# LSTM over 512 steps with a residual: opening matmuls, head sums on GpSimd, and the order of loads at the end

## The chip, the cores and the metric

The kernel runs on one core of a Trainium2 chip. The core has five engines that work at the same time, each with its own stream of instructions: PE (TensorE, matmuls), DVE (VectorE), ACT (ScalarE), POOL (GpSimd) and SP (SyncE, which here only issues DMAs). They wait for each other by semaphores. All arithmetic is in float32. The metric is the device time of one execution in microseconds.

## The reference

```python
xW = jnp.einsum('ntd,dg->ntg', x, Wx) + b       # x: (32, 512, 512), Wx: (512, 2048)
def step(carry, xw_t):
    prev_h, prev_c = carry
    a = xw_t + prev_h @ Wh                       # Wh: (512, 2048)
    i = sigmoid(a[:, :Hd]);  f = sigmoid(a[:, Hd:2 * Hd])
    o = sigmoid(a[:, 2 * Hd:3 * Hd]);  g = tanh(a[:, 3 * Hd:])
    next_c = f * prev_c + i * g
    next_h = o * tanh(next_c)
    return ((next_h, next_c), next_h)
_, hs = jax.lax.scan(step, (h0, zeros), swapaxes(xW, 0, 1))
out = x + swapaxes(hs, 0, 1)                     # batch 32, 512 steps, width 512
```

Two matrix products carry the arithmetic: x by Wx, which does not depend on the recurrence, and h by Wh, which must be done step after step.

## The kernel before

**Two kinds of PE work.** In every step t, `h_part(t)` (L245) adds h by Wh into the step's PSUM bank `gbank`; the profile shows it as 32 records of 128x512 elements. The product x by Wx is made ahead of the recurrence and put between the h_parts, so that PE has work while ACT and DVE run the step's `cell` (L260 to L271: sigmoids, tanh, products, and a transpose that gives the new h, `ht`). GpSimd adds x to h for the output (`oc`, L279).

**The stream.** For steps 20 to 499, x by Wx is computed with a fast bilinear algorithm that needs fewer products. The steps come in 20 groups of 24; a group has 20 slots, a slot seven products (L516). Each product has

- a left operand, a sum of rows of x: rows are loaded into `xs` (L475, alternately in `xs0` and a part of `r1`), four "pair sums" per group (`pair_sum`, L480 to 486, 128x768) follow, then "U sums" (`u_op`, L424, 128x896, into the six buffers of `ubuf`, made by `u_ahead` as far as the next matmuls need them);
- a right operand, a sum of blocks of Wx ("V rows"), made once in the first 90 us, stored to `vdram` and read back row by row into the three places of `vring` (L595, `load_v_ahead`), always three rows at most.

The products gather in five PSUM banks `xbank` and in `bbank`. `evacuate` (L562 to 578) copies and adds them into `cbuf`; `needs` says which evacuation must have been issued before a bank is used again. "W sums" (`w_op`, L389, 128x1024 in `cbuf`) then form the blocks of x by Wx, which are stored to `xwd` (L405) and come back per step into `xw` (L613, four loads, three steps ahead); ACT copies `xw` into the bank of the next step (`seed_step`, L624). Some banks start from a bias row rather than from zero: `seed_banks` (L546) copies one of six "seeds". The six are differences of the four bias rows in two halves; two are made early (`early_seeds`), four late (`late_seeds`: three 256 KB loads by POOL at L729, three splits L733, three sums L741 to 743 on DVE).

**The head.** Steps 0 to 19 use plain products (`plain_block`, L178): those of five steps stand ahead of the loop, the rest in the loop's steps 0 to 7. Before those, a loop of three rounds with four matmuls each (L795) multiplies a zeroed tile into banks that are not in use yet. From step 7 on the head's steps run the stream, in chunks of up to 24 quarter products; each chunk loads V rows, makes U sums, evacuates, makes W sums as long as the budget `room["dve"]` lasts, and issues the matmuls; after the first chunk of a step comes its `cell`.

**The main loop and the end.** From step 16 on each step has one run of stream matmuls, and the same calls in a fixed order: evacuate, seeds, V loads, U sums, pair sums, W sums, matmuls, cell. The stream ends at step 472 (`END`) and 473; steps 500 to 511 use plain products again (`plain_part`, L187), which are put into steps from 472 on, 10 per step until `SPLIT` (474) and 5 after. From 474 on a step's gates are worked on in two halves. The x rows for the output come in chunks of eight steps (`load_x`, L151); the last chunk is loaded into a place that served as a spare `cbuf` buffer.

**The order** of each engine's instructions is the order of these calls: nothing reorders them. SP issues all DMAs but three, in one queue; an issue whose data or place is not ready holds up every issue behind it. At the end of a step's `h_part`, SP gets the stores of the step before, then the x chunk if one is due, the `xw` loads, and later the V loads.

Of the kernel before, what the change touches and what calls it, by code (L numbers as in the profile page):

```python
# [12 lines left out]
P = 128  # L13
# [7 lines left out]
W = G * P  # L21
HW = G * H
# [56 lines left out]
def cost_dve(cols):  # L79
    return 150 + 1.05 * cols  # L80
# [17 lines left out]
def kernel(  # L98
# [193 lines left out]

    free_c = list(range(NC))
    last_x = []
    free_u = list(range(6))
    room = {"dve": 0.0}
# [5 lines left out]
    def flat(a):  # L304
        return a.rearrange("p a b -> p (a b)")
# [110 lines left out]
    def u_block(gr, i):  # L416
        if i < 6:
            return flat(xs[gr.g % 2][:, i, 1:8])
        return flat(ubuf[:, gr.u[i]])

    def u_op(gr, terms):
        (a, sa), (b, sb) = sorted(terms.items(), key=lambda v: -v[1])
        dst = take(free_u)
        (add if sb > 0 else sub)(flat(ubuf[:, dst]), u_block(gr, a), u_block(gr, b))  # L424
        room["dve"] -= cost_dve(896)
        for i in (a, b):
            if i > 5:
                gr.u_uses[i] -= 1
                if gr.u_uses[i] == 0:
                    free_u.append(gr.u[i])  # L430
        return dst

    u_made = [0]

    def make_sum(gr, i):
        if i > 5 and i not in gr.u:
# [36 lines left out]
            in_=xg[g].rearrange("p (k s m) -> p k s m", k=6, s=4),  # L473
        )

    def pair_sum(g, i):
        z = xs[g % 2]
        a21, a11, a12, a22, s1, s2, s3, s4 = (z[:, :, n] for n in range(8))
        if i == 0:
            add(s1, a21, a22)  # L480
        elif i == 1:
            sub(s2, s1, a11)
        elif i == 2:
            sub(s3, a11, a21)
        else:
            sub(s4, a12, s2)
        room["dve"] -= cost_dve(768)
# [5 lines left out]
                items.append((row, row - back, r))  # L493
    pos = [0]
    finished = []

    def emit_matmuls(n):

        while n > 0 and pos[0] < 4 * len(items):
            i, q = divmod(pos[0], 4)  # L500
            row, slot, r = items[i]
            gr, s = group(slot // R), slot % R
            xb = xbank[slot % 5]
            if q == 0 and any(f in finished for f in needs(slot, r)):
                evacuate()
            if r == 2:
                dst = bbank[:, slot % 2 * HW : (slot % 2 + 1) * HW]
            elif r in (5, 3):
                dst = xb[:, HW:W]
            else:  # L510
                dst = xb[:, 0:HW]
            start = q == 0 and (r == 2 or (r == 1 and s not in BIAS_OF))
            size = 4 if q == 0 and n >= 4 else 2
            cols = slice(q * HW // 4, (q + size) * HW // 4)
            for j in range(4):
                nc.tensor.matmul(  # L516
                    dst[j * B : (j + 1) * B, cols],
                    left_of(gr, s, r)[:, j * B : (j + 1) * B],
                    vring[:, row % 3, RIGHT[r], cols],
                    start=start,  # L520
                    stop=True,
                    skip_group_check=True,
                )
            pos[0] += size
            n -= size
            if pos[0] % 4 == 0:
                finished.append((slot, r))
                if r == 4:
                    left_done(gr, s)
# [205 lines left out]
    def early_seeds():  # L735
        split_seeds((4, 5))
        sub(seeds[5], seeds[5], seeds[4])

    def late_seeds():
        split_seeds((0, 1, 2))  # L740
        add(seeds[3], seeds[2], seeds[4])  # L741
        sub(seeds[2], seeds[2], seeds[0])
        sub(seeds[1], seeds[1], seeds[0])

# [23 lines left out]
    with tc.manual_schedule():  # L770
# [19 lines left out]
        load_x(1)  # L790
        load_x(0, 5, 8)
        load_x(2, 0, 4)
        for n in range(3):
            for j in range(NJ):
                nc.tensor.matmul(  # L795
                    xbank[1 + n % 2][j * B : (j + 1) * B],
                    tanh_c[:, 0:B],
                    tanh_c.unsqueeze(1).to_broadcast([P, 4, P]),
                    start=True,
                    stop=True,  # L800
                )
# [10 lines left out]
        jobs = {}  # L812
        for t, ss in enumerate(V_STEPS):
            jobs.setdefault(t, []).extend([lambda s=s: v_slot(s) for s in ss])
        jobs.setdefault(6, []).extend([lambda i=i: pair_sum(0, i) for i in range(4)] + [early_seeds])
        dve_jobs = []

        HEAD_STEPS = STREAM0
# [1 line left out]
        done_work = 0.0  # L820
        n_plain = 0
        group_loaded = 1
        late_seeds_due = [late_seeds]
        plains_done = T
        s_done = {0: 4}
        v_ready = False
# [6 lines left out]
        for t in range(T):  # L833
# [10 lines left out]
                free_c.append(NC)  # L844
            if t >= SPLIT - 16 and not last_x and NC in free_c:
                free_c.remove(NC)
                load_x(NCHUNK - 1)
                last_x.append(t)
            assert last_x or t < SPLIT - 4
            if t == 3:  # L850
                load_x(2, 4, 8)
                load_seeds(((4, 3), (5, 1)), nc.sync)
                load_group(0)
            if PARKED <= t + 3 < HEAD + NG * GS:
                load_xw(t + 3)

            if t < HEAD_STEPS:
                target = head_work * (t + 1) / HEAD_STEPS
                chunks = []
                for p in HEAD_PLAINS[t] if t < len(HEAD_PLAINS) else ():  # L860
                    chunks.append(("plain", p))
                    n_plain += 1
                    done_work += PLAIN
                n = 4 * int((target - done_work) / PROD + 0.5) if n_plain == HEAD - KEPT else 0
                if t == HEAD_STEPS - 1 and n:
                    n = R * 7 * 4 - pos[0]
                left = n
                while left > 0:
                    m = min(left, 24)
                    chunks.append(("stream", m))  # L870
                    left -= m
                done_work += n * PROD / 4
                todo = jobs.pop(t, [])
                plains = sum(k == "plain" for k, _ in chunks)
                for i, (kind, m) in enumerate(chunks):
                    if kind == "plain":
                        bank = bank_of(m) if m < STRAIGHT else park_bank(m)
                        room["dve"] = 3000.0
                        for cc in range(4):
                            plain_block(m, cc, bank)  # L880
                        if i == 0:
                            cell(t)
                            if t + 1 >= STRAIGHT:
                                seed_step(t + 1)
                        keep(m)
                        if n_plain == HEAD - KEPT:
                            plains_done = t
                        last = i == plains - 1
                        for _ in range(len(todo) if last else -(-len(todo) // (plains - i))):
                            todo.pop(0)()  # L890
                            flush_v()
                    else:
                        load_v_ahead()
                        u_ahead(m)
                        room["dve"] = m * PROD / 4 * 1.5
                        evacuate()
                        if late_seeds_due and plains_done < t - 1:
                            late_seeds_due.pop()()
                        if t >= HEAD_STEPS - 3 and dve_jobs:
                            dve_jobs.pop(0)()  # L900
                        u_ahead(m + 24)
                        while wqueue and room["dve"] > 0:
                            w_op()
                        seed_banks(m)
                        emit_matmuls(m)
                        if i == 0:
                            cell(t)
                            if t + 1 >= STRAIGHT:
                                seed_step(t + 1)
                            if t == plains_done + 1:  # L910
                                load_seeds(((0, 0), (1, 1), (2, 2)), nc.gpsimd)
                if t >= 5:
                    load_v_ahead()
                if t >= 10 and group_loaded == 1 and n_plain == HEAD - KEPT and not dve_jobs and not jobs:
                    assert not v_stores
                    load_group(1)
                    group_loaded = 2
                    dve_jobs += [lambda i=i: pair_sum(1, i) for i in range(4)]
                continue


# [2 lines left out]
                max(0, min(R * 7 * 4 + (t + i - STREAM0) * R * 7 * 2 // GS * 2, 4 * len(items)) - pos[0]) for i in (1, 2)  # L924
            )
            n = target
            room["dve"] = 3800.0 + min(0.0, room["dve"])
            evacuate()
            seed_banks(n)
# [17 lines left out]
            if t in LATE:  # L947
                late_loads.pop(0)()
            emit_matmuls(n)
            kept_late = []  # L950
            due = 0 if t < END else 10 if t < SPLIT else 5
            while due and plain_tail:
                p, c, q = plain_tail[0]
                m = 2 if due > 1 and q % 2 == 0 else 1
# [65 lines left out]
```

## Time and profile before

| what | value |
|---|---|
| runs | 3124.54, 3127.91, 3130.99 us (median 3127.91) |
| profiled execution, its own time | 3126.34 us |
| its span in the trace | 3124.6 us |
| PE busy / DVE / ACT / POOL | 3097.0 / 2232.2 / 1451.1 / 234.9 us |
| stream matmuls (L516) start at | about 107 us |
| last `h_part` starts at | 3116.25 us |

The profile prints for each engine how long it was busy, in groups of equal instructions, and what ended the idle time before them: "idle before <-DVE cbuf L568" means that the engine stood still until that DVE instruction was done. Windows show the same for stretches of time, with the TensorE clock that was granted (1.00 is full) and the share of time in which the DMA engines were busy. Matmul records overlap their predecessors, so a record's duration is longer than the distance to the next one. A matmul instruction leaves two records.

### The profile page before, as it was taken

What the parts mean: (1) busy time and instruction counts of PE and PEld (TensorE: products, weight loads), DVE (VectorE), ACT (ScalarE), POOL (GpSimd) and SP (SyncE); (2) the same over time, 40 slices, a digit from 0 to 9 for tenths busy, and PEclk for the clock granted to TensorE, in tenths of its full rate; (3) what the DMA queues carried; (4) which work ended last, traced back from release to release, by engine and by line L of the source; (5) the groups of instructions that cost most, each with busy time, mean ns of one, the idle gap of its engine ahead of it and who ended that gap; (6) DMA issues with size and microseconds to landing.
All of it is one profiled execution on the core that took longest, in us unless ns stands there. A gap on an engine that the chain in (4) does not pass through costs nothing.

```text
span 3124.6 us, 109095 instructions
## 1 busy us (share of the span) xinstructions
PE 3097.0 (99%) x44032; PEld 1664.7 (53%) x44032; DVE 2232.2 (71%) x6217; ACT 1451.1 (46%) x5483; POOL 234.9 (8%) x511
## 2 busy tenths in 40 slices
PE   9999999999999999999999999999999999999999
PEld 6544555555555555555555555555555555555576
DVE  6686777767676767777676767677776767676644
ACT  1244444444444444444444444444444444444444
POOL 0000000000000000000000000000000000000010
PEclk9999999999999999999999999999999999999999
DMA  9687878787878778787778787787877787878630
GB/s 353 220 300 233 260 245 272 231 253 239 261 242 267 243 246 263 244 276 230 253 243 259 245 264 242 247 267 239 276 231 251 244 258 246 267 240 275 195 92 21
DMA packets 307368, 760.37 MB, mean 243 GB/s; under 512 B 49008, under 2 KB 91760, under 8 KB 306352
## 3 DMA queue, kind: packets, MB, share of 16 engines
q1 hardware_dynamic: 306624, 752.61, 76.5%
q8 instruction: 347, 5.69, 0.8%
q14 instruction: 157, 1.29, 0.1%
q0 software_dynamic: 240, 0.79, 0.1%
HBM read 573.90 MB, written 179.31 MB: 241 GB/s over the span
## 4 chain that ended last, share of the span: by engine, by line
PE 96%; DVE 2%; DMA 1%; ACT 1%; issue 0%; SPq 0%; POOL 0%; DVEq 0%; ACTq 0%
PE gbank L245 53%; PE xbank L516 32%; PE bbank L516 5%; PE xbank L245 3%; PE xbank L187 1%; PE xbank L178 1%; PE gbank L178 1%; DMA vring<-vdram 1%; PE bbank L178 0%; DVE cbuf L389 0%; DVE prod L264 0%; DMA r<-in_L_cond_b_dram 0%; DMA r<-in_L_cond_Wx_dram 0%; DVE s L265 0%; DVE ubuf L424 0%
## 5 line engine op out<-in xcount | busy, mean ns | idle before, releaser
L245 PE MATMUL gbank<-wh_sb,ht 128*32 128x512 f32 (+1 forms) x16224 | 1779.8, 577 | 2.8 <-DVE hbuf L269 1.3
L245 PEld LDWEIGHTS gbank<-wh_sb,ht 128*32 128x32 f32 x16224 | 610.7, 110 | 827.1 <-issue 709.0
L516 PE MATMUL xbank<-vring,ubuf 128*32 128x256 f32 (+1 forms) x15464 | 958.6, 365 | 8.1 <-issue 2.4
L260 ACT ACTIVATE s<-gbank 128x128 f32<-128x128 f32 x976 | 274.1, 281 | 1279.8 <-PE gbank L245 1279.3
L516 PEld LDWEIGHTS xbank<-vring,ubuf 128*32 128x32 f32 x15464 | 587.3, 110 | 374.1 <-issue 192.9
L264 DVE TENSOR_TENSOR prod<-s 128x128 f32<-128x128 f32 x1024 | 293.9, 287 | 629.9 <-ACT s L261 629.6
L389 DVE TENSOR_TENSOR cbuf<-cbuf 128x1024 f32<-128x1024 f32 x408 | 491.0, 1216 | 1.4
L279 POOL TENSOR_TENSOR oc<-xnat,ht 128x128 f32<-128x128 f32 x504 | 233.0, 462 | 2851.3 <-DVE ht L271 1336.5
L267 ACT ACTIVATE tanh_c<-s 128x64 f32<-128x64 f32 x1024 | 262.4, 256 | 248.2 <-DVE s L265 243.6
L271 DVE STREAM_TRANSPOSE ht<-hbuf 128x64 f32<-128x64 f32 x1022 | 250.8, 245 | 75.4 <-DVE hbuf L269 2.3
L624 ACT COPY gbank<-xw 128x512 f32<-128x512 f32 x463 | 278.8, 602 | 0.1
L265 DVE TENSOR_TENSOR s<-prod 128x64 f32<-128x64 f32 x1024 | 230.3, 225 | 35.2
L562 ACT COPY cbuf<-xbank 128x512 f32<-128x512 f32 x374 | 218.5, 584 | 44.9 <-PE xbank L516 31.2
L269 DVE TENSOR_TENSOR hbuf<-o,tanh_c 128x64 f32<-128x64 f32 x1024 | 213.1, 208 | 29.0 <-ACT tanh_c L267 28.5
L261 ACT ACTIVATE s<-gbank 128x64 f32<-128x64 f32 x976 | 226.0, 232 | 0.0
L572 DVE TENSOR_TENSOR cbuf<-xbank,cbuf 128x256 f32<-128x256 f32 x374 | 153.3, 410 | 77.4 <-ACT cbuf L571 74.0
L516 PE MATMUL bbank<-vring,ubuf 128*32 128x256 f32 (+1 forms) x2704 | 200.9, 356 | 3.3 <-DVE cbuf L568 3.3
L516 PE MATMUL xbank<-vring,r 128*32 128x256 f32 (+1 forms) x2480 | 173.5, 372 | 3.1 <-DMA vring<-vdram 3.1
L516 PE MATMUL xbank<-vring,xs 128*32 128x256 f32 (+1 forms) x2472 | 173.2, 373 | 0.4 <-DMA vring<-vdram 0.2
L262 ACT ACTIVATE o<-gbank 128x128 f32<-128x128 f32 (+1 forms) x507 | 155.2, 306 | 0.0
L568 DVE TENSOR_TENSOR cbuf<-bbank,cbuf 128x256 f32<-128x256 f32 x374 | 151.6, 405 | 3.0 <-PE bbank L516 3.0
L575 DVE TENSOR_TENSOR cbuf<-xbank,cbuf 128x256 f32<-128x256 f32 x374 | 152.0, 406 | 0.0
(104 smaller groups left out, 1798.3 us busy)
## 6 DMA issues: line engine op xcount, KB each, us to landing
vring<-vdram SPq DMA_DIRECT2D x340, 896.0 KB, 6.6
xw<-xwd SPq DMA_DIRECT2D x1920, 64.0 KB, 4.2
xwd<-cbuf SPq DMA_DIRECT2D x221, 512.0 KB, 7.6
out_dram<-oc SPq DMA_DIRECT2D x255, 128.0 KB, 3.2
xnat<-in_x_dram SPq DMA_DIRECT2D x62, 512.0 KB, 5.3
xs<-in_x_grouped_dram SPq DMA_DIRECT2D x10, 1536.0 KB, 10.7
vring<-vdram SPq DMA_DIRECT2D x20, 768.0 KB, 6.6
r<-in_x_grouped_dram SPq DMA_DIRECT2D x10, 1536.0 KB, 10.8
```

The costliest lines, as they stand in the source:

```text
L245: nc.tensor.matmul(dst[j * B : (j + 1) * B], state["ht"][:, k], m, start=False, stop=True, skip_group_check=True)
L260: nc.scalar.activation(s[:, u, 0:2], g[:, n_, 0:2], AF.Sigmoid)
L261: nc.scalar.activation(s[:, u, 2], g[:, n_, 3], AF.Tanh)
L264: nc.vector.tensor_mul(prod[:, u], s[:, u, 0:2], s[:, u, 2:4])
L265: add(nxt[:, u, 3], prod[:, u, 0], prod[:, u, 1])
L267: nc.scalar.activation(tanh_c[:, HALVES[u]], nxt[:, u, 3], AF.Tanh)
L271: nc.vector.transpose(ht[:, 2 * u : 2 * u + 2].rearrange("p q b -> p (q b)"), hbuf[:, HALVES[u]])
L279: (nc.gpsimd if t < T - 8 else nc.vector).tensor_add(oc[:, tt % 2], x_of(t), ht)
L389: op(c_of(dst), c_of(src), c_of(bb))
L516: nc.tensor.matmul(dst[j * B : (j + 1) * B, cols], left_of(gr, s, r)[:, j * B : (j + 1) * B], vring[:, row % 3, RIGHT[r], cols], start=sta ...
L562: nc.scalar.copy(t[:, 0:4:3], xb.rearrange("p (n c) -> p n c", n=2))
L624: nc.scalar.copy(bank_of(t), src)
```

## The change

Seven edits, at the opening, in the head, and at the end:

1. The opening loop runs six rounds rather than three.
2. In the head (`in_head`), U sums run on GpSimd rather than on VectorE; the first of them are asked for in step 6. So do group 1's four pair sums.
3. The seeds: three raw bias rows are loaded on SP's queue in step 5 into `cbuf` buffers 8 and 9 (`free_c` hands these out last), split on GpSimd in step 6, and `late_seeds` forms three seeds on GpSimd and one by a copy on ACT. The POOL-issued loads fall away.
4. The head's stream runs in chunks of 12 rather than 24 when other chunks stand before them, with the budget for W sums carried from chunk to chunk.
5. In the main loop V rows are loaded once more after a step's matmuls have been issued (`load_v_ahead()`), ahead of the next step's stores, x chunk and `xw` loads.
6. The last x chunk is loaded three steps later than the point at which its place becomes free.
7. From step 470 on, `emit_matmuls` returns (`wait_at_end`) where it used to evacuate in the middle; what is left goes into the next step, and the step's plain parts are cut by as many (`max(0, 10 - n)`).

```diff
@@ -292,7 +292,7 @@
-    free_c = list(range(NC))
+    free_c = [*range(8), 10, 8, 9]
     last_x = []
     free_u = list(range(6))
     room = {"dve": 0.0}
@@ -421,8 +421,10 @@
     def u_op(gr, terms):
         (a, sa), (b, sb) = sorted(terms.items(), key=lambda v: -v[1])
         dst = take(free_u)
-        (add if sb > 0 else sub)(flat(ubuf[:, dst]), u_block(gr, a), u_block(gr, b))
-        room["dve"] -= cost_dve(896)
+        eng = nc.gpsimd if in_head[0] else nc.vector
+        (eng.tensor_add if sb > 0 else eng.tensor_sub)(flat(ubuf[:, dst]), u_block(gr, a), u_block(gr, b))
+        if not in_head[0]:
+            room["dve"] -= cost_dve(896)
         for i in (a, b):
             if i > 5:
                 gr.u_uses[i] -= 1
@@ -431,6 +433,7 @@
         return dst
     u_made = [0]
+    in_head = [True]
     def make_sum(gr, i):
         if i > 5 and i not in gr.u:
@@ -473,8 +476,9 @@
             in_=xg[g].rearrange("p (k s m) -> p k s m", k=6, s=4),
         )
-    def pair_sum(g, i):
+    def pair_sum(g, i, eng=nc.vector):
         z = xs[g % 2]
+        add, sub = eng.tensor_add, eng.tensor_sub
         a21, a11, a12, a22, s1, s2, s3, s4 = (z[:, :, n] for n in range(8))
         if i == 0:
             add(s1, a21, a22)
@@ -493,6 +497,7 @@
                 items.append((row, row - back, r))
     pos = [0]
     finished = []
+    wait_at_end = [False]
     def emit_matmuls(n):
@@ -502,6 +507,8 @@
             gr, s = group(slot // R), slot % R
             xb = xbank[slot % 5]
             if q == 0 and any(f in finished for f in needs(slot, r)):
+                if wait_at_end[0]:
+                    return
                 evacuate()
             if r == 2:
                 dst = bbank[:, slot % 2 * HW : (slot % 2 + 1) * HW]
@@ -736,11 +743,20 @@
         split_seeds((4, 5))
         sub(seeds[5], seeds[5], seeds[4])
+    def load_raw_seeds():
+        for i in range(3):
+            nc.sync.dma_start(out=parks[i], in_=bias[i : i + 1].to_broadcast([P, W]))
+
+    def split_raw_seeds():
+        for q in parks[0:3]:
+            nc.gpsimd.tensor_sub(q[:, HW:W], q[:, HW:W], q[:, 0:HW])
+
     def late_seeds():
-        split_seeds((0, 1, 2))
-        add(seeds[3], seeds[2], seeds[4])
-        sub(seeds[2], seeds[2], seeds[0])
-        sub(seeds[1], seeds[1], seeds[0])
+        q = parks
+        nc.gpsimd.tensor_add(seeds[3], q[2], seeds[4])
+        nc.gpsimd.tensor_sub(seeds[2], q[2], q[0])
+        nc.gpsimd.tensor_sub(seeds[1], q[1], q[0])
+        nc.scalar.copy(seeds[0], q[0])
@@ -790,7 +806,7 @@
         load_x(1)
         load_x(0, 5, 8)
         load_x(2, 0, 4)
-        for n in range(3):
+        for n in range(6):
             for j in range(NJ):
                 nc.tensor.matmul(
                     xbank[1 + n % 2][j * B : (j + 1) * B],
@@ -812,7 +828,10 @@
         jobs = {}
         for t, ss in enumerate(V_STEPS):
             jobs.setdefault(t, []).extend([lambda s=s: v_slot(s) for s in ss])
-        jobs.setdefault(6, []).extend([lambda i=i: pair_sum(0, i) for i in range(4)] + [early_seeds])
+        jobs.setdefault(6, []).extend(
+            [lambda i=i: pair_sum(0, i) for i in range(4)]
+            + [early_seeds, split_raw_seeds, lambda: u_ahead(28)]
+        )
         dve_jobs = []
         HEAD_STEPS = STREAM0
@@ -820,7 +839,6 @@
         done_work = 0.0
         n_plain = 0
         group_loaded = 1
-        late_seeds_due = [late_seeds]
         plains_done = T
         s_done = {0: 4}
         v_ready = False
@@ -844,13 +862,16 @@
                 free_c.append(NC)
             if t >= SPLIT - 16 and not last_x and NC in free_c:
                 free_c.remove(NC)
+                last_x.append(t)
+            if last_x and t == last_x[0] + 3:
                 load_x(NCHUNK - 1)
-                last_x.append(t)
             assert last_x or t < SPLIT - 4
             if t == 3:
...
                 load_seeds(((4, 3), (5, 1)), nc.sync)
                 load_group(0)
+            if t == 5:
+                load_raw_seeds()
             if PARKED <= t + 3 < HEAD + NG * GS:
                 load_xw(t + 3)
@@ -866,7 +887,7 @@
                     n = R * 7 * 4 - pos[0]
                 left = n
                 while left > 0:
-                    m = min(left, 24)
+                    m = min(left, 12 if chunks else 24)
                     chunks.append(("stream", m))
                     left -= m
                 done_work += n * PROD / 4
@@ -892,30 +913,31 @@
                     else:
                         load_v_ahead()
                         u_ahead(m)
-                        room["dve"] = m * PROD / 4 * 1.5
+                        if i == 0:
+                            room["dve"] = min(room["dve"], 1000.0) + PLAIN
                         evacuate()
-                        if late_seeds_due and plains_done < t - 1:
-                            late_seeds_due.pop()()
                         if t >= HEAD_STEPS - 3 and dve_jobs:
                             dve_jobs.pop(0)()
                         u_ahead(m + 24)
-                        while wqueue and room["dve"] > 0:
+                        while wqueue and room["dve"] > 800:
                             w_op()
                         seed_banks(m)
                         emit_matmuls(m)
+                        room["dve"] += m * PROD / 4
                         if i == 0:
                             cell(t)
+                            room["dve"] -= 2500.0
                             if t + 1 >= STRAIGHT:
                                 seed_step(t + 1)
                             if t == plains_done + 1:
-                                load_seeds(((0, 0), (1, 1), (2, 2)), nc.gpsimd)
+                                late_seeds()
                 if t >= 5:
                     load_v_ahead()
...
                     load_group(1)
                     group_loaded = 2
-                    dve_jobs += [lambda i=i: pair_sum(1, i) for i in range(4)]
+                    dve_jobs += [lambda i=i: pair_sum(1, i, nc.gpsimd) for i in range(4)]
                 continue
@@ -924,6 +946,8 @@
                 max(0, min(R * 7 * 4 + (t + i - STREAM0) * R * 7 * 2 // GS * 2, 4 * len(items)) - pos[0]) for i in (1, 2)
             )
             n = target
+            in_head[0] = False
+            wait_at_end[0] = t >= END - 2
             room["dve"] = 3800.0 + min(0.0, room["dve"])
             evacuate()
             seed_banks(n)
@@ -947,8 +971,9 @@
             if t in LATE:
                 late_loads.pop(0)()
             emit_matmuls(n)
+            load_v_ahead()
             kept_late = []
-            due = 0 if t < END else 10 if t < SPLIT else 5
+            due = 0 if t < END else max(0, 10 - n) if t < SPLIT else 5
             while due and plain_tail:
                 p, c, q = plain_tail[0]
                 m = 2 if due > 1 and q % 2 == 0 else 1
```

## The prediction

> **What bounds the kernel now.** I read the page's busy times first, then what TensorE waited for, then windows, and last the timelines around each wait.
>
> ```profile
> span 3124.6 us, 109095 instructions
> PE 3097.0 (99%) x44032; PEld 1664.7 (53%) x44032; DVE 2232.2 (71%) x6217; ACT 1451.1 (46%) x5483; POOL 234.9 (8%) x511
> PE bbank L516 <- DVE cbuf L568: 3.3, 2, 1.8
> PE xbank L516 <- DMA vring<-vdram: 3.3, 3, 2.1
> PE gbank L245 <- DVE hbuf L269: 1.3, 1, 1.3
> PE xbank L516 <- DVE cbuf L572: 1.2, 1, 1.2
> PE gbank L245 <- DVE ht L271: 1.1, 2, 0.8
> PE xbank L245 <- DVE ht L271: 0.7, 1, 0.7
> PE xbank L516 <- DVE cbuf L575: 0.4, 1, 0.4
> ```
>
> TensorE is busy 99%; the waits (total, times, longest) and an uneven clock are all that can be won without taking work away. 3124.6 - 3097.0 leaves 27.6 us idle. The windows (length, busy time and count of each engine, granted clock, DMA share, GB/s) say where:
>
> ```profile
> 0.00:20.00 20.00, 15.71 (x200) 9.13 (x201) 8.63 (x9) 1.59 (x2) 0.20 (x4) 0.91 0.93 322
> 100.00:200.00 100.00, 89.39 (x1331) 44.63 (x1325) 74.39 (x161) 38.38 (x120) 5.41 (x11) 0.98 0.67 233
> 120.00:140.00 20.00, 16.88 (x248) 8.34 (x244) 14.04 (x32) 5.59 (x19) 2.39 (x5) 0.91 0.64 230
> 400.00:2900.00 2500.00, 2499.01 (x34652) 1314.01 (x34648) 1837.01 (x5117) 1207.90 (x4509) 192.40 (x419) 1.00 0.81 251
> 2900.00:2950.00 50.00, 46.02 (x612) 22.90 (x608) 33.37 (x92) 19.00 (x76) 5.33 (x8) 0.97 0.69 221
> 5.54:8.95 3.41, 0.74 (x8) 0.99 1.03 386
> 8.95:12.36 3.41, 3.39 (x34) 0.51 1.05 397
> 12.36:15.78 3.42, 3.42 (x68) 1.00 1.12 322
> 2900.04:2903.45 3.41, 1.27 (x32) 0.99 0.99 378
> 2903.45:2906.87 3.42, 3.42 (x24) 0.51 1.00 285
> ```
>
> The 2500 us in the middle lose 0.99 (PE's is the second number). The head from 100 to 200 loses 100 - 89.4 = 10.6, the opening 4.3, the end of the stream 4.0. The last five rows show TensorE alone: after 3.41 us in which it was busy for only 0.74, or 1.27, the clock is about half for the next 3.41 us: 34 records instead of 68, a loss of 1.7. The clock of 0.91 from 120 to 140 is a third such case (0.09 x 20 = 1.8). So 27.6 + 1.7 + 1.7 + 1.8 = 32.8 us is the ceiling.
>
> **Opening (gain 0.8).** Three more rounds are 12 matmuls, 24 records.
>
> ```profile
> 1.60 4.68 PE L795 MATMUL xbank<-tanh_c 128*32 128x512 f32 x24 [1.60 <-DVE tanh_c L772]
> 8.97 3.56 PE L178 MATMUL gbank<-r,xnat 128*32 128x256 f32 x32 [2.69 <-DMA r<-in_L_cond_Wx_dram]
> 31.31 5.00 PE L178 MATMUL xbank<-r,xnat 128*32 128x256 f32 x88
> 18.81 1.36 SPq L151 DMA_DIRECT2D xnat<-in_x_dram  x3
> DMA to landing us min/median/max: 3.0/11.7/11.9
> ```
>
> At full clock 68 records of 256 columns take 3.42 us, 0.05 each, so 0.10 each for 512 columns and 2.4 for 24: they end at 6.28 + 2.4 = 8.7, inside the wait for Wx. If instead they go at the first rounds' 4.68 / 24 = 0.195, they end at 11.0, 2.0 late. I take the first, since the slow records were the earliest. The window before 8.95 is then full and the half clock should fall away: 1.7. But the start feeds on DMAs that do not move (DMA share 1.0): the x chunk issued at 18.81 lands some 11.7 later, 30.5, and is used at 31.31. Only 0.8 of the 1.7 survives. Bounds -2.0 and +1.7. The Trainium skill ("TensorE: Matmul & The Clock Gate", Part 1) calls the window 3413 ns long and free-running, not tied to the kernel's start; by that the wait for Wx would spoil a window in some runs only, and the gain on another run would be anything between 0 and 1.7. The trace agrees on the length (the two stretches of half clock above) and cannot show the phase of other runs.
>
> **First U sums (gain 1.8).** The stream's first product waits for a U sum:
>
> ```profile
> 109.22 1.07 PE L516 MATMUL xbank<-vring,ubuf 128*32 128x256 f32 x16 [1.82 <-DVE ubuf L424]
> 108.08 2.08 DVE L424 TENSOR_TENSOR ubuf<-xs 128x896 f32<-128x896 f32 x2
> 147.39 3.73 DVE L389 TENSOR_TENSOR cbuf<-cbuf 128x1024 f32<-128x1024 f32 x3
> 195.42 2.35 DVE L389 TENSOR_TENSOR cbuf<-cbuf 128x1024 f32<-128x1024 f32 x2
> 2937.34 2.58 DVE L389 TENSOR_TENSOR cbuf<-cbuf 128x1024 f32<-128x1024 f32 x2
> 2937.57 1.28 POOL L279 TENSOR_TENSOR oc<-xnat,ht 128x128 f32<-128x128 f32 x1 [8.05 <-DVE ht L271]
> L279 POOL TENSOR_TENSOR oc<-xnat,ht 128x128 f32<-128x128 f32 x504 | 233.0, 462 | 2851.3 <-DVE ht L271 1336.5
> ```
>
> Both sums stood on DVE behind step 7's cell and a bias addition. On POOL they stand behind three splits only, and need group 0's pair sums, which the order puts into step 6. What do they cost there? No trace row has a U sum on POOL. Below: DVE's own 2.08 / 2 = 1.04. Above: POOL's 0.46 for 128 columns in proportion, 3.2. The last rows show how the two engines collide: POOL's 128-column sum took 1.28 instead of 0.46 beside two W sums on DVE, and those two took 2.58 instead of 2.35. So one waits for the other, and 128 POOL columns hold DVE 0.23. I read 0.23 fixed and 0.23 per 128 columns (together the 0.46): 1.84 for 896, 1.6 for 768, 1.15 for 512, 0.7 for 256, and take these, since they split 0.46 by rows that show both engines. Three splits and one sum make 3.9; step 6's pair sums come a whole step before 109.22 - 1.82 = 107.4, when the product wants its operand: the wait goes. Bounds 0 and 1.8.
>
> **Late seeds (gain 4.8, cost 1.5).** DVE's splits of the seeds and what TensorE did meanwhile:
>
> ```profile
> L733 DVE TENSOR_TENSOR r<-r x3: 424/424/426, 124.8 to 129.7; 128x256 f32<-128x256 f32 x3
> DMA r<-in_L_cond_b_dram: 4.2, 3
> 133.29 1.07 PE L516 MATMUL xbank<-vring,ubuf 128*32 128x256 f32 x16 [2.44 <-issue]
> 134.99 2.65 PE L516 MATMUL xbank<-vring,ubuf 128*32 128x256 f32 x24 [0.63 <-ACT cbuf L562]
> ```
>
> From 124.8 to 129.7 DVE stands in L733, 4.2 of it waiting for three loads in turn, with the seeds' sums, a U sum and evacuations behind it. TensorE then runs dry for 2.4 and 0.6 and pays 1.8 of half clock. The new loads go out on SP in step 5 instead of step 8, and no DVE instruction waits for them. But the three seeds (3 x 1.15 = 3.5) now stand on POOL ahead of two U sums. I charge 1.5, between 0 and 3.5.
>
> **Rest of the head (gain 2.8, cost 1.5).** What is left of the 10.6 is 10.6 - 1.8 - 3.0 = 5.8: two waits for L568 (3.3), one for L572 (1.2), small ones for ACT. Evacuations were due while DVE was in W or U sums: three W sums at 147.39 take 3.73, two at 195.42 take 2.35. The change takes 15 U sums, four pair sums of 768 columns, three splits of 0.42 and three seeds of 512 columns off DVE; with 1.04 per 896 columns that is 15.6 + 3.6 + 1.3 + 1.8 = 22.3 us, and with chunks of 12 evacuates twice as often. But three W sums can still stand in a row, and each POOL sum can now stop one. I take half, 2.8, as gone and charge 1.5 for one new wait of that kind; bounds +5.8 and -20 (the first rival).
>
> **V loads and the end of the stream (gain 6.8).**
>
> ```profile
> 2894.26 0.34 SPq L151 DMA_DIRECT2D xnat<-in_x_dram  x1
> 2896.56 0.37 SPq L595 DMA_DIRECT2D vring<-vdram  x1
> vring<-vdram SPq DMA_DIRECT2D x340, 896.0 KB, 6.6
> 281.47 1.07 PE L516 MATMUL xbank<-vring,r 128*32 128x256 f32 x16 [0.98 <-DMA vring<-vdram]
> 2903.12 0.45 PE L516 MATMUL xbank<-vring,r 128*32 128x128 f32 x8 [2.14 <-DMA vring<-vdram]
> ```
>
> The V row that TensorE wanted at 2900.98 was issued at 2896.56 and took its usual 6.6. Ahead of it in SP's queue were the x chunk and four `xw` loads. Now it goes ahead of both, as soon as its place in `vring` is free: if that is by 2894.26, 2.3 earlier, and the wait of 2.1 goes, with the 1.7 of half clock after it. Of the two other V waits (3.3 - 2.1 = 1.2) the one at 281 stands in the same loop, after the same order: 1.0. What queues behind a V load that waits for TensorE are stores and `xw` loads, and these have three steps in hand. Letting go at step 470 instead of evacuating puts the last cell ahead of three evacuations: of the 0.4 + 1.3 I keep 1.3, since 20 quarter products are less cover than 24. And the plain parts that slide one step later fill one of the three gaps of the last steps (1.1 + 0.7): 0.7. Sum 2.1 + 1.7 + 1.0 + 1.3 + 0.7 = 6.8; bounds 0 and 7.3.
>
> **Sum.** 0.8 + 1.8 + 4.8 - 1.5 + 2.8 - 1.5 + 6.8 = 14.0. The profiled execution took 3126.3, 1.6 below the median of 3127.9; 3112.3 on its footing, 3114 against the median.
>
> **Rivals.**
>
> *GpSimd blocks VectorE (slower, 10%).* In the head POOL gets 15 U sums, 4 pair sums, 3 seeds and 3 splits: 27.6 + 6.4 + 3.5 + 2.1 = 40 us by my prices, 48 + 11 + 5.5 + 2.8 = 67 by the upper ones. DVE was idle 100 - 74.4 = 25.6 of the 100 us and gets 22.3 back: 48 in all. If every POOL sum stops DVE for its whole length, 40 still fits and 67 overruns by 19. The point is 48 us, a U sum of 2.3. Beyond, evacuations run late all through the head: +19, none of the head's gains, and 7.6 from opening and end: 3127.9 + 11.4 = 3139. For it: the 1.28 row. Against: the price would have to be near the upper one, and DVE's evacuations have one input from PSUM. The Trainium skill ("SBUF — State Buffer", "Who interferes with whom") has the two engines share a port pair as a lock held for a whole instruction, and only DVE instructions with two SBUF inputs contend. By that W sums and cells would wait and evacuations would not, and the overrun of 19 would shrink; the trace agrees on the waiting (1.28 for 0.46), and no row of it shows an evacuation beside a long POOL sum.
>
> *The head only moves its waits (18%).* New waits for POOL's U sums cost what the three parts from the first U sums on win; opening, V loads and end keep 7.6: 3120. For it: U sums nearly twice as long at 1.84 as at 1.04. Against: POOL was busy 5.4 of the 100 us.
>
> *Early V loads do not help (8%).* They may be late for the DMA engines' sake (share 0.99 in that window) rather than by issue. Then 14.0 - 2.1 - 1.7 - 1.0 = 9.2: 3119; with the opening's 0.8 lost too and a second new head wait of 1.5, 3121.
>
> *The change does nothing that shows (8%).* Waits removed here are paid at the next late DMA or evacuation: 3125 to 3128.
>
> **How the numbers follow.** My own case has 56%, with 3106 to 3119. About 0.2%, 6.3 us, is what a measurement can tell from no change, so faster means under 3121.7. Faster: 56 + 17 of the 18 + 5 of the 8 (its values lie close to the line) = 78%. Same: 1 + 3 + 8 = 12%. Slower 10%. The range starts at 3105: all head waits and both charges gone (3.0 + 3.0), the full opening (0.9) and the end's bound (0.5) make 7.4 more than the sum, 3107, and runs lie up to 3 from their median. It ends at 3127, which leaves out the slower rival and little else.
>
> **What would show it.** Right: the windows 100 to 200 with under 6 us idle and no clock of 0.91; L795 running on to about 8.7 and a full window from 8.95; no L733 wait on DVE; no V wait at 2901 and a clock of 1.00 from 2900 to 2950; POOL's U sums at 1.8 to 2.0. Wrong: L424 on POOL over 2.3, TensorE waiting for `ubuf` from POOL more than twice, DVE W sums in the head well above 1.2, or the idle time of the middle above 1.

## The result and the profile after

The changed kernel takes 3120.16 us (median of 7 runs, 3118.84 to 3121.53); the kernel before, beside it, 3129.57 (7 runs). The ratio is 0.9973, interval 0.9961 to 0.9984: faster by 0.15 to 0.4%. The forecast was 3114, the range 3105 to 3127. The number came out within the range, but by luck: two errors of opposite sign met. The head, which was to win 6.4, lost 6.4, and the main loop, given nothing, won 4.1 between the two profiled executions. The second rival's figure, 3120, is the measured one, but it had the head at nothing won and nothing lost, so that is luck as well.

The page's span and busy times of the changed kernel:

```profile
span 3119.8 us, 109182 instructions
PE 3094.5 (99%) x44064; PEld 1660.0 (53%) x44064; DVE 2226.7 (71%) x6192; ACT 1452.0 (47%) x5484; POOL 282.0 (9%) x533
```

Its list of what TensorE waited for (total, times, longest; line numbers are the changed kernel's: L523 was L516, L425 was L424, L575 and L579 were L568 and L572):

```profile
PE bbank L523 <- DVE cbuf L575: 7.3, 3, 3.8
PE xbank L523 <- POOL ubuf L425: 3.2, 2, 1.6
PE xbank L523 <- ACT xbank L553: 2.4, 3, 1.0
PE xbank L523 <- DVE cbuf L579: 2.4, 1, 2.4
```

Its windows, with the columns as before:

```profile
0.00:20.00 20.00, 18.41 (x252) 10.81 (x256) 7.86 (x9) 1.59 (x2) 0.20 (x4) 1.00 0.92 313
100.00:200.00 100.00, 87.79 (x1308) 43.06 (x1299) 66.47 (x135) 38.50 (x120) 46.89 (x29) 0.98 0.65 223
140.00:160.00 20.00, 16.59 (x244) 7.58 (x239) 14.68 (x31) 7.92 (x26) 5.65 (x5) 0.91 0.76 270
200.00:260.00 60.00, 56.73 (x776) 25.21 (x780) 41.07 (x107) 25.75 (x92) 7.20 (x10) 0.97 0.86 282
400.00:2880.00 2480.00, 2479.85 (x34444) 1308.71 (x34437) 1824.41 (x5086) 1200.63 (x4478) 191.52 (x417) 1.00 0.78 252
2900.00:2950.00 50.00, 49.52 (x720) 26.84 (x716) 35.54 (x102) 22.06 (x91) 4.97 (x9) 1.00 0.71 221
```

All V waits are gone from the list, and the end and the opening run at full clock. But 100 to 200 us is idle for 12.2 instead of 10.6, 200 to 260 for 3.3 instead of none, and two windows pay for a half clock (0.91 of 20 us, 0.97 of 60; before, one did, from 120 to 140).

Idle time does not tell where the whole difference lies; the starts of the steps' h_parts do. Each number below is worked out from the two records that begin a stretch and end it, such as these of step 45 and step 466 in TensorE's timeline before:

```profile
383.85 0.64 PE L245 MATMUL gbank<-wh_sb,ht 128*32 128x512 f32 x4
2895.18 1.07 PE L245 MATMUL gbank<-wh_sb,ht 128*32 128x512 f32 x8
```

and in the timeline after:

```profile
389.09 1.49 PE L245 MATMUL gbank<-wh_sb,ht 128*32 128x512 f32 x11
2896.32 1.07 PE L245 MATMUL gbank<-wh_sb,ht 128*32 128x512 f32 x8
```

| stretch | before | after | won | forecast |
|---|---|---|---|---|
| to step 1 | 38.22 | 38.27 | -0.05 | 0.8 |
| steps 1 to 17 (head) | 177.31 | 183.73 | -6.4 | 1.8 + 3.3 + 1.3 = 6.4 |
| 17 to 45 (wait at 281) | 168.32 | 167.09 | 1.2 | 1.0 |
| 45 to 466 (main loop) | 2511.33 | 2507.22 | 4.1 | 0 |
| 466 to 468 (wait at 2901) | 15.88 | 11.84 | 4.0 | 3.8 |
| 468 to 511 (end) | 205.18 | 203.28 | 1.9 | 2.0 |

That is 4.8 between two single executions. Of the 9.4 between medians the rest is that the profiled execution of before was 3.2 better than the median of 3129.57, and the one after 1.4 worse than its own.

### The profile page after: what moved, and what is told of

Read it like the earlier page. It is cut to its first block, busy times and chain, and to the rows that moved or that the text cites. A ratio compares the mean times of both kernels' runs of the same rounds, so it can differ in the third digit from the quotient of the medians.

```text
span 3119.8 us, 109182 instructions
## 1 busy us (share of the span) xinstructions
PE 3094.5 (99%) x44064; PEld 1660.0 (53%) x44064; DVE 2226.7 (71%) x6192; ACT 1452.0 (47%) x5484; POOL 282.0 (9%) x533
## 4 chain that ended last, share of the span: by engine, by line
PE 94%; DVE 1%; issue 1%; ACT 0%; POOL 0%; DVEq 0%; ACTq 0%; POOLq 0%
PE gbank L245 53%; PE xbank L523 32%; PE bbank L523 5%; PE xbank L245 2%; PE xbank L187 1%; DVE cbuf L389 0%; DVE prod L264 0%; DVE s L265 0%; POOL ubuf L425 0%; ACT s L260 0%; DVE hbuf L269 0%; DVE ht L271 0%; ACT tanh_c L267 0%; POOL r L486 0%; ACT gbank L631 0%
## 5 line engine op out<-in xcount | busy, mean ns | idle before, releaser
L523 PE MATMUL xbank<-vring,ubuf 128*32 128x256 f32 (+1 forms) x15464 | 955.2, 364 | 6.2 <-POOL ubuf L425 3.2
L523 PEld LDWEIGHTS xbank<-vring,ubuf 128*32 128x32 f32 x15464 | 585.3, 110 | 371.7 <-issue 190.6
L389 DVE TENSOR_TENSOR cbuf<-cbuf 128x1024 f32<-128x1024 f32 x408 | 503.2, 1246 | 1.7 <-ACT cbuf L585 0.2
L579 DVE TENSOR_TENSOR cbuf<-xbank,cbuf 128x256 f32<-128x256 f32 x374 | 153.3, 410 | 76.7 <-ACT cbuf L578 74.7
L523 PE MATMUL bbank<-vring,ubuf 128*32 128x256 f32 (+1 forms) x2704 | 200.1, 355 | 7.3 <-DVE cbuf L575 7.3
L523 PE MATMUL xbank<-vring,xs 128*32 128x256 f32 (+1 forms) x2472 | 172.9, 373 | 1.8 <-ACT xbank L553 1.8
L523 PE MATMUL xbank<-vring,r 128*32 128x256 f32 (+1 forms) x2480 | 173.2, 372 | 0.0
L575 DVE TENSOR_TENSOR cbuf<-bbank,cbuf 128x256 f32<-128x256 f32 x374 | 151.5, 405 | 0.0
```

The costliest lines, as they stand in the source:

```text
L389: op(c_of(dst), c_of(src), c_of(bb))
L523: nc.tensor.matmul(dst[j * B : (j + 1) * B, cols], left_of(gr, s, r)[:, j * B : (j + 1) * B], vring[:, row % 3, RIGHT[r], cols], start=sta ...
```

## The experiments

All are compared with the kernel before, measured beside them, by medians of 5 to 12 runs (15 or 23 of the kernel before); "steps 1 to 17" and the like are read from one trace each. The kernel before had medians of 3127.2 to 3129.6 in these comparisons, so a difference between kernels that were not measured side by side is less sure.

**The edits one at a time.** The extra V load alone (`v_load_alone`):

```diff
             emit_matmuls(n)
+            load_v_ahead()
             kept_late = []
```

> The kernel before with edit 5 alone: V rows are loaded once more right after a step's matmuls. Theory (early issue): the V waits go, the one at 281 us (1.0), the one at 2901 (2.1) with its half clock (1.7), and some 24 short ones in the main loop that the step lengths of the two traces show (a step of 6.02 us taking up to 6.4; 4.3 us from step 44 to 461): 8 to 10 us faster than before, with the step at 2865 us reached 5 us earlier. Rival (the DMA engines are the limit, not the issue): 0 to 3 us faster, the short waits still there.

3116.22 us, ratio 0.9959 (0.9946 to 0.9972): 11.6 faster, above theory's 8 to 10, and faster than all seven edits together (3120.16, though not measured beside it). Its waits of TensorE from 200 to 2950 us are two:

```profile
PE gbank L245 <- DVE hbuf L269: 1.3, 1, 1.3
PE xbank L516 <- DVE cbuf L575: 0.4, 1, 0.4
```

Steps 45 to 466 take 2508.1. The three kernels below that lack the extra load (`opening_alone`, `end_alone`, `x_late_alone`) took 2515.0, 2518.5 and 2521.3 there, the kernel before 2511.3; all nine profiled kernels with it take 2507.2 to 2508.2. So the main loop lost 3 to 13 us, another amount in each of four executions, and edit 5 takes all of it.

The opening alone (`opening_alone`, `range(3)` to `range(6)`):

> The kernel before with edit 1 alone: six opening rounds. Theory (the start is bound by its DMAs): L178 starts at full clock and step 0's h_part comes 1.5 us earlier (26.4), then waits about 0.9 for the last Wh block; step 1's h_part stays within 0.2 of 38.22, and the time within 1 us. Rival (the prediction): 0.8 us stay, step 1 at 37.4.

3128.31 against 3127.85, ratio 1.0004 (0.9994 to 1.0015). Step 1 came at 36.59, outside the theory's 0.2; but it came at 37.05 with the old opening in the next experiment, and at 38.27 with the new one in the changed kernel. One trace says nothing here: the first load of Wx lands anywhere from 6.86 to 8.84 us in the 13 traces of this case, a spread wider than what the edit could win. Over these 13, step 1 comes at 36.59 to 38.54 with six rounds (eight traces, mean 37.70) and at 37.05 to 38.33 with three (five, mean 37.87).

The end alone (`end_alone`, edits 6 and 7):

> The kernel before with edits 6 and 7 alone (last x chunk three steps later; waiting at the end of the stream). Theory: 2.4 us from the last stream steps (waits for L575 and hbuf), the V wait at 2901 stays at 1 to 2 us with its half clock: 2 to 3 us faster. Rival (the second x chunk is what makes the V row late): the wait at 2901 goes too, 6 us faster.

3122.72, ratio 0.9984 (0.9974 to 0.9994): 5.1 faster. Steps 466 to 468 take 11.84: the rival was right, the V wait goes without the extra V load. (The time alone would not tell, since the main loop varies by more.) A later run with edit 6 alone, `x_late_alone`, names the cause:

```diff
             if t >= SPLIT - 16 and not last_x and NC in free_c:
                 free_c.remove(NC)
-                load_x(NCHUNK - 1)
                 last_x.append(t)
+            if last_x and t == last_x[0] + 3:
+                load_x(NCHUNK - 1)
```

> The kernel before with edit 6 alone (last x chunk three steps later). Theory (that x chunk stands in SP's queue until the store out of its place has landed, some 6 us, with the V load behind it): the wait at 2901 and its half clock go, steps 466 to 468 in 11.8 us instead of 15.9; 3 to 4.5 us faster than before. Rival (end_alone owed this to the waiting at the end): no change.

3123.70, ratio 0.9989 (0.9980 to 0.9998), 3.8 faster, steps 466 to 468 in 11.84. The timeline of SP's queue in the kernel before shows why:

```profile
2887.79 0.39 SPq L405 DMA_DIRECT2D xwd<-xnat  x1
2894.26 0.34 SPq L151 DMA_DIRECT2D xnat<-in_x_dram  x1
```

The same store in the list of DMAs that it issued from 2885 to 2935 (count, size, us to landing):

```profile
xwd<-xnat SPq DMA_DIRECT2D x1, 512.0 KB, 6.5
```

And SP's own waits from 2885 to 2900:

```profile
SPq L151 <- DMA xwd<-xnat: 6.0, 1, 6.0
```

The x chunk goes into the place that this store reads, so it went out 2894.26 - 2887.79 = 6.5 us after it, the store's whole time to landing; for 6.0 of these SP stood still, with four `xw` loads and the V load behind it. Edit 5 cures the same wait by putting the V load first. Either alone would have done for it.

**The head.** Everything but the head's edits (`old_head`: 1, 5, 6, 7):

> The kernel before with edits 1, 5, 6 and 7, so with the head's sums, seeds and chunks as before. Theory (the head's edits cost 6 to 7 us by the step times: step 16 starts at 216.2 in the changed kernel against 209.7): 14 to 16 us faster than before, 5 to 7 us faster than the changed kernel. Rival (the head's edits gain, as predicted): 6 us slower than the changed kernel.

3114.87, ratio 0.9956 (0.9944 to 0.9967): 13.0 faster than before, a little under theory's 14, against 9.4 for the changed kernel in its own comparison. Steps 1 to 17 are back at 177.4. The head's edits cost, as a whole. Which?

From the changed kernel, the later U sums and group 1's pair sums go back to VectorE (`sums_on_dve`):

```diff
-        eng = nc.gpsimd if in_head[0] else nc.vector
+        eng = nc.gpsimd if on_pool[0] else nc.vector
...
+            if t == 8:
+                on_pool[0] = False
...
-                    dve_jobs += [lambda i=i: pair_sum(1, i, nc.gpsimd) for i in range(4)]
+                    dve_jobs += [lambda i=i: pair_sum(1, i) for i in range(4)]
```

> The changed kernel, with the head's U sums from step 8 on and group 1's pair sums on VectorE again; U sums still uncharged in the W sums' budget, first U sums, seeds and chunks of 12 as changed. Theory (GpSimd's long sums and DVE's W sums stop each other in turn): W sums in the head go back from 1.85 to about 1.22 us, TensorE's waits for L575 (7.3) and L579 (2.4) mostly go, steps 1 to 17 take 171 to 175 us instead of 183.7; 8 to 12 us faster than the changed kernel, about 3110. Rival (the chunks and the uncharged budget put W sums ahead of evacuations): W sums at 1.22, but the waits stay, steps 1 to 17 at 180 or more.

3106.37, ratio 0.9936 (0.9923 to 0.9948): 20.9 faster than before and 13.8 faster than the changed kernel. Steps 1 to 17 take 169.6 instead of 183.7, below what theory gave. The window 100 to 200 of this kernel:

```profile
100.00:200.00 100.00, 94.85 (x1448) 48.15 (x1443) 78.72 (x169) 42.63 (x135) 13.07 (x14) 1.00 0.73 253
```

Its W sums from 100 to 210, in the groups by shape (busy, mean ns):

```profile
L389 DVE TENSOR_TENSOR cbuf<-cbuf 128x1024 f32<-128x1024 f32 x23 | 27.9, 1218 | 0.2
```

The same group in the changed kernel:

```profile
L389 DVE TENSOR_TENSOR cbuf<-cbuf 128x1024 f32<-128x1024 f32 x18 | 33.2, 1853 | 0.3 <-ACT cbuf L585 0.2
```

VectorE has more to do now (78.7 us busy against 66.5), and TensorE waits 5.5 us less than before (5.15 against 10.6) and 7.1 less than in the changed kernel. The changed kernel's 18 W sums had taken 33.2 us instead of 18 x 1.22 = 21.9.

The other half of the pair, sums left on GpSimd and the old chunks and budget back (`old_chunks`):

```diff
-                    m = min(left, 12 if chunks else 24)
+                    m = min(left, 24)
...
+                        room["dve"] = m * PROD / 4 * 1.5
-                        while wqueue and room["dve"] > 800:
+                        while wqueue and room["dve"] > 0:
```

> The changed kernel with the head's chunks of 24 and the old budget for W sums; sums and seeds on GpSimd as changed. Theory (GpSimd): the waits for evacuations stay within 3 us of the changed kernel's, steps 1 to 17 at 181 to 187 us, 3118 to 3123. Rival (the chunks): steps 1 to 17 at 178 or less, 3114 or less.

3121.07, ratio 0.9980 (0.9971 to 0.9989), steps 1 to 17 in 183.6: the chunks are not the cause. With both put back, so that only seeds and first U sums differ from before in the head (`sums_dve_old_chunks`):

> The changed kernel with the head as before except for the seeds and the first U sums, which stay on GpSimd. Theory: the wait of 1.8 at 107 and the 4.8 of the late seeds go, nothing else moves: steps 1 to 17 in 170 to 173 us instead of 177.3, 3108 to 3111. Rival (evacuations queue for other reasons and the head only moves its waits): 176 to 178, 3114 to 3116.

3108.75, ratio 0.9944 (0.9931 to 0.9957), steps 1 to 17 in 171.7. That is 12.3 faster than `old_chunks`, measured beside it: with either kind of chunk the sums on GpSimd cost 12 to 14 us. It is 2.4 slower than with small chunks, their budget and U sums that are not charged to it; which of the three wins that is not shown. The same with the first U sums on VectorE too (`seeds_alone`, `in_head = [False]`):

> As the kernel before this one (head as before except for the seeds), with the first U sums on VectorE in step 6 too. Theory (the first U sums need only to be made early, by either engine): within 1 us of it. Rival (GpSimd is what takes the first U sums out of the way): 1 to 2 us slower, with TensorE waiting for L425 from DVE or a later V store.

3108.44, ratio 0.9941 (0.9928 to 0.9953). The first U sums had only to be asked for in step 6; the engine did not matter. Against `old_head` the seeds and the early U sums win 6.4 (3114.87 - 3108.44; 6.2 by steps 1 to 17, 177.4 against 171.2).

**The best version, and the opening again.** `sums_on_dve` with the first U sums on VectorE:

> sums_on_dve with the first U sums on VectorE too, so that only seeds and splits are on GpSimd. Theory (the first U sums need only be made early): within 1.5 us of sums_on_dve, 3105 to 3108. Rival (GpSimd's free time is worth having for sums that stand beside no W sum): 2 us or more slower.

3105.55, ratio 0.9933 (0.9920 to 0.9947), the fastest kernel of the study, 22 us below before. And `sums_on_dve` with the old opening:

> sums_on_dve with three opening rounds as before. Theory (the DMAs of the start take back what the opening wins): within 0.7 us of sums_on_dve, and step 1's h_part at 37 to 38.4 in both. Rival (the prediction): 0.8 us slower or more.

3107.34, ratio 0.9939 (0.9927 to 0.9952), 1.0 slower than `sums_on_dve`, which favours the rival. But the two were not measured side by side, their runs overlap (3106.34 to 3108.03 against 3105.91 to 3106.71), step 1 came at 37.57 here and at 37.84 in `sums_on_dve`, as theory had it, and `old_head`, which has the new opening, did not come out lower than its other parts explain: `v_load_alone` less the 1.9 that `old_head` wins from step 468 on would be 3114.3, and it took 3114.87. These three comparisons give the opening -0.5, -0.5 and +1.0 us; what it is worth stays open.

## Why the prediction came out as it did

- **Opening (0.8).** The clock went as said: no half clock follows the six rounds, in this trace or in the seven others that have them. The loop is longer than the 8.7 that I gave it: TensorE goes from it to the first product at 9.09 without a wait, though Wx had landed at 8.45 (before, the product began 0.13 after the landing). In `old_head` Wx was in at 6.86 and the product began at 9.52, so there the rounds themselves held TensorE up. What survives is not settled. In the changed kernel's trace nothing did: step 0 began 1.52 earlier, and the last block of Wh, which I had not put a time to, took 0.9 of it back. TensorE's timeline of the changed kernel:

```profile
1.59 7.67 PE L811 MATMUL xbank<-tanh_c 128*32 128x512 f32 x48 [1.59 <-DVE tanh_c L788]
9.09 1.96 PE L178 MATMUL gbank<-r,xnat 128*32 128x256 f32 x32
```

and its list of waits:

```profile
PE gbank L245 <- DMA wh_sb<-in_L_cond_Wh_dram: 0.9, 1, 0.9
```

- **First U sums (1.8) and late seeds (4.8).** Right together: 6.6 forecast, 6.4 measured where nothing else in the head was changed. The reason given for the first, GpSimd's freedom, was beside the point: `seeds_alone` makes them on VectorE.
- **The charge for POOL in the late seeds (1.5).** Right: TensorE waits 1.62 at 125.06 for the U sum behind the three seeds (the changed kernel's timeline):

```profile
125.06 0.64 PE L523 MATMUL xbank<-vring,ubuf 128*32 128x256 f32 x8 [1.62 <-POOL ubuf L425]
```

- **Rest of the head (2.8 - 1.5).** This step failed, and it is the mechanism that failed: I charged 1.5 for one new wait behind a stopped W sum, and took half of the old waits as gone. In the runs the sums on GpSimd cost 13.8 us (3120.16 - 3106.37), by the traces 14.1 in steps 1 to 17. Against `sums_on_dve` the changed kernel's trace has 7.7 more in waits for the evacuations L575 and L579 (9.7 against 2.0), 3.2 in waits for U sums from POOL (1.6 of them the charge above) and two stretches of half clock at 1.7 each. One of my signs of being wrong showed it: W sums in the head well above 1.2, at 1.85. My single POOL sum was not far off (1.84 against 2.1 when alone, 2.3 on average). The slower rival set its point at a total of 48 us, a U sum of 2.3; by its own list the total was 50.5 (34.5 + 9.3 + 3.9 + 2.9), so by its account 2 to 3 us should have run over (the lengths include what POOL itself stood for VectorE). But the totals were the wrong thing to add up: VectorE was idle for 33.5 of the 100 us, and TensorE waited for it all the same. The timelines of VectorE and GpSimd in the changed kernel, with the matmul that waited:

```profile
157.99 5.43 DVE L389 TENSOR_TENSOR cbuf<-cbuf 128x1024 f32<-128x1024 f32 x2
157.22 5.12 POOL L425 TENSOR_TENSOR ubuf<-xs,ubuf 128x896 f32<-128x896 f32 x2
164.14 0.64 PE L523 MATMUL bbank<-vring,ubuf 128*32 128x256 f32 x8 [2.68 <-DVE cbuf L575]
196.35 2.11 POOL L425 TENSOR_TENSOR ubuf<-ubuf 128x896 f32<-128x896 f32 x1
197.20 5.35 DVE L389 TENSOR_TENSOR cbuf<-cbuf 128x1024 f32<-128x1024 f32 x2
198.42 3.05 POOL L425 TENSOR_TENSOR ubuf<-r 128x896 f32<-128x896 f32 x1
203.27 0.64 PE L523 MATMUL bbank<-vring,ubuf 128*32 128x256 f32 x8 [3.82 <-DVE cbuf L575]
```

Two W sums take 5.4 instead of 2.35, because a POOL sum takes the turn before each: the first pair of POOL sums ends at 159.31 and 162.34, the W sums beside it end at 160.39 and 163.42. The evacuations that TensorE needs stand behind the W sums in VectorE's order, and TensorE waits 2.68 and 3.82. A queue of one engine pays for each stop at once; free time later in the 100 us is no use to it. By the rival's own words (evacuations late all through the head) it was the case that happened, at 14 us rather than 19, and the other edits paid for it.
- **V loads (2.1 + 1.7 + 1.0).** Right in size (4.0 and 1.2 in the table), and early issue rather than the DMA engines' share was the limit, as `v_load_alone` shows. The cause at 2901 was only half seen: I had the x chunk ahead of the V load, not that it stood there waiting for a store.
- **The middle ("loses 0.99").** Wrong: it lost 3 to 13. Here is one such wait, in TensorE's timeline of step 99 in the kernel before:

```profile
706.14 3.65 PE L245 MATMUL gbank<-wh_sb,ht 128*32 128x512 f32 x32
711.73 1.07 PE L516 MATMUL xbank<-vring,xs 128*32 128x256 f32 x16 [0.21 <-DMA vring<-vdram]
712.59 0.64 PE L245 MATMUL gbank<-wh_sb,ht 128*32 128x512 f32 x4
```

The step takes 712.59 - 706.14 = 6.45 instead of the 6.02 of most, so about 0.42 are lost, and the profile shows 0.21: the records before a wait are drawn about 0.2 longer than the distance to their successors, and a short wait hides in that. Against the same steps of `v_load_alone`, 15 steps of the loop are longer, by 0.04 to 0.42 and 3.2 in all; in the three other executions without the extra load it is 15, 20 and 26 steps, by up to 1.9. I read the idle time of one execution, not the lengths of the steps.
- **End (1.3 + 0.7).** Right: 1.9 in all, though split otherwise. Step 471 shrinks from 8.21 to 5.78: its waits fall by 1.4 (0.44 + 1.34 to 0.41), and 16 plain records of 0.05 move behind step 473, where the steps take 0.5 longer rather than 0.8 (177.13 against 176.62 up to the last `h_part` record). So the gaps took in about 0.3 of the plain parts, not 0.7. With edit 6 alone (`x_late_alone`) step 471 keeps 8.21, so this is edit 7's.

## What to carry to other kernels

Before a sum is moved to GpSimd, look at which sums of VectorE with two operands in SBUF it will run beside, and what waits behind these in VectorE's order: each can wait for the other's whole length, and a budget over a stretch does not see it. In a queue of DMA issues, look for the issue that cannot go yet: the loads behind it are late however short they are. In a loop that TensorE fills, compare the lengths of the steps; the idle column can miss half of each short wait and all of its variation between runs.

## What the runs showed of the hardware

Evacuations, which read one operand from PSUM, are not stopped by GpSimd here. In the changed kernel two of them run at their usual 0.41 beside the POOL sum at 184.44, while the first product of a cell, whose two operands are in SBUF, took 1.41 instead of 0.29 at 192.86, beside the one at 192.03 (the changed kernel's timelines):

```profile
184.47 0.41 DVE L582 TENSOR_TENSOR cbuf<-xbank,cbuf 128x256 f32<-128x256 f32 x1
184.81 0.41 DVE L575 TENSOR_TENSOR cbuf<-bbank,cbuf 128x256 f32<-128x256 f32 x1
184.44 2.08 POOL L425 TENSOR_TENSOR ubuf<-ubuf,xs 128x896 f32<-128x896 f32 x1
192.03 2.09 POOL L425 TENSOR_TENSOR ubuf<-xs 128x896 f32<-128x896 f32 x1
192.86 1.41 DVE L264 TENSOR_TENSOR prod<-s 128x128 f32<-128x128 f32 x1 [1.82 <-ACT s L261]
```

The Trainium skill ("SBUF — State Buffer", "Who interferes with whom") has VectorE contend with GpSimd only in instructions with two SBUF inputs or in a two-port mode. Here the traces bear out the first on both sides (0.41 beside a POOL sum, 1.41 for 0.29), and no run here shows the second. The evacuations themselves were spared, and they were late all the same, by their place in the order.

The half clock of the opening does not come with every execution: with the same three rounds `end_alone` had a wait of 1.68 for Wx and ran its first 32 products in 1.97 us, the kernel before one of 2.69 and 3.56. TensorE's timeline of `end_alone`:

```profile
7.39 1.97 PE L178 MATMUL gbank<-r,xnat 128*32 128x256 f32 x32 [1.68 <-DMA r<-in_L_cond_Wx_dram]
```

Of the five traces with three rounds the half clock came in the three with waits of 2.03 to 2.69, and not in the two with 1.51 and 1.68. The length of a wait is not all that decides, as the clock records of the traces show; the prediction had left this open. Within one trace all stretches of half clock begin on one grid: before, at 8.89, 135.19 and 2903.39, which is 37 and 848 times 3.4133 us from the first; in the changed kernel at 149.67 and 204.28, 16 times 3.4133 apart. From one execution to the next the grid lies elsewhere: 2.06 us from the start of the span before, 2.89 in the changed kernel, 1.22 in `v_load_alone`. So what a wait costs depends also on where it falls. TensorE's waits of 2.22 and 0.62 in the head of `v_load_alone` (at 133 us) were followed by 3.41 us of half clock, and those of 2.27 and 0.63 at the same place in `opening_alone` by none.
